# Moving the sums of a layer norm from VectorE to ScalarE in 36 of 64 gates

## The chip, the cores and the metric

The kernel runs on one core of a Trainium2 chip, in float32. A core has a matrix engine (TensorE, "PE" in the profile; its weight loads are shown apart as "PEld"), three engines for elementwise work (VectorE "DVE", ScalarE "ACT", GpSimd "POOL"), and SyncE ("SP"), which issues transfers. Each engine works through a queue of its own, in order; the engines wait for each other through semaphores. The metric is the device time of one execution in microseconds (us). The time before is 2115.55 us, the median of three runs (2112.75, 2115.55, 2115.77).

## The reference

64 graphs of 256 nodes with 256 features each go through two layers of a graph network, each closed by a layer norm over the features. Cut to what matters:

```python
def _layernorm(x, axis=-1, eps=1e-5):
    m = jnp.mean(x, axis=axis, keepdims=True)
    v = jnp.var(x, axis=axis, keepdims=True)
    return (x - m) / jnp.sqrt(v + eps)

# layer 0: normalized adjacency times x times W, residual, norm
x = _layernorm(x + L0(x, adj, W, b, alpha))

# layer 1: a convolution over the nodes, message passing, and a GRU cell, residual, norm
h = relu(bn1(conv1d(x, conv1_w)))                      # 1 tap
x_conv = relu(bn2(conv1d(h, conv2_w)) + x)             # 17 taps
A = exp(-dist(x @ w_se.T + b_se)) * adj
x_nmp = A @ relu(x @ w_msg.T + b_msg)
x_in = concatenate([x_conv, x_nmp])
gi = x_in @ w_ih.T + b_ih
gh = x @ w_hh.T + b_hh
r, z = sigmoid(gi_r + gh_r), sigmoid(gi_z + gh_z)
n = tanh(gi_n + r * gh_n)
x = _layernorm(x + (1 - z) * n + z * x)
```

The change concerns the last line alone: how the mean and the variance of each node's 256 features are formed.

## The kernel before

**Quarters.** The 64 graphs are worked on in four quarters of 16 (Q). The convolution of 17 taps is done in a frequency domain: each graph is cut into 8 tiles of 32 nodes and transformed by matmuls, and a quarter's 16 x 8 tiles fill 128 partitions. So each quarter goes through: `layer0` and `layer1` graph by graph (layer1 ends in the tile's transform and in `xn_d`, the message-passing result in DRAM); 12 frequency steps (matmuls L548, whose weights `u` are streamed from DRAM by SP; the results are taken out of PSUM by ScalarE, L590, and VectorE, L592 and L593); an inverse transform, which is VectorE's work alone (L598, L630, L735 and their like); and then the gates, one GRU cell per graph.

**The gate stage.** `gru(g)` (L858) works on one graph in four pieces, each ended by a `yield`, at which other work may be put between. Its matrix product is formed by seven products of three matmuls of 384 columns each (L874), after a scheme of Strassen's kind, so sums of the inputs are needed beside them; POOL makes these (`sums`, L845) for the next graph. VectorE adds the products into `G` (L891, L892, L901, L903, L941), ScalarE copies two of them (L885, L894) and takes the tanh (L916, L932), VectorE does the arithmetic of the gates (`finished`, L924 to L934). L934 leaves the value to be normed in the tile that the profile calls `x_g` (256 nodes as 128 partitions x 2 chunks x 256 features). The input of the next graph gets its two relu passes on ScalarE in piece 3 (`transposed`, L823 or L831).

**The norm.** `normed` (L849) calls `layernorm` (L319): per chunk VectorE's statistics (`bn_stats` L326) and their aggregate (`bn_aggr` L327), then for both chunks the variance plus eps (L328, VectorE), the power -1/2 (L329, POOL), minus mean times that (L332, VectorE), and on ScalarE the application (L334). L852 issues the store of the result on ScalarE's queue. It is a generator with a halt after L329: `finished` runs it up to there, `ended()` (L854) runs the rest, in piece 3 of the next graph's gate, ahead of that graph's own load of x1 (`load_x1`, L801, on SP's queue). The tile for x1, which becomes `x_g`, has two buffers.

**Where gates run.** `gates(q, part)` chains gates. The first four of each quarter (EARLY, L772) run beside the layers of the next quarter's graphs. Gates 4 to 15 of the first three quarters are put into the next quarter's work: up to two in the frequency steps (pieces of a gate between steps), then `paced` beside the inverse transform (for each marked instruction of the main stream so many pieces of the other one are put behind it; RATES, L1096), and what is left beside the layers of the quarter after. The last quarter's 16 gates run alone at the end. The gates that stand fully beside the last quarter's inverse transform are 37 to 44.

**What sets the order.** The order of the calls is a program order; a scheduler then orders each engine's queue by its own estimates, and only `tc.issue_after` fixes places. So the order in a queue may differ from that of the text.

Of the kernel before, what the change touches and what calls it, by code (L numbers as in the profile page):

```python
# [9 lines left out]
F32 = mybir.dt.float32  # L10
AF = mybir.ActivationFunctionType
ALU = mybir.AluOpType
AX = mybir.AxisListType

P = 128
LN_EPS = 1e-5
# [10 lines left out]
def kernel(  # L27
# [27 lines left out]
    nc = tc.nc  # L55
    B, N, D = x.shape
# [3 lines left out]
    NCH = N // P  # L60
# [7 lines left out]
    Q = P // GT  # L68
# [11 lines left out]
    small = ctx.enter_context(tc.tile_pool(name="small", bufs=4))  # L80
# [4 lines left out]
    def accbank(name):  # L85
        return psacc.tile([P, 512], F32, tag="acc", name=name)
# [4 lines left out]
    def mark(op, gates=0):  # L91
        marks.append((op.ins, gates))
# [27 lines left out]
    unused = const.tile([P, N], F32, name="unused")  # L120
    neg_half = const.tile([P, 4], F32)
# [197 lines left out]
    def layernorm(y, eps=LN_EPS):  # L319

        chunks = range(y.shape[1])
        st = small.tile([P, NCH, nc.vector.BN_STATS_DIM], F32, name="ln_st")
        mv = small.tile([P, NCH, nc.vector.BN_AGGR_DIM], F32, name="ln_mv")
        rs = small.tile([P, NCH], F32, name="ln_rs")
        for c in chunks:
            nc.vector.bn_stats(st[:, c, :], y[:, c, :])  # L326
            nc.vector.bn_aggr(mv[:, c, :], st[:, c, :])  # L327
        nc.vector.tensor_scalar(rs[:, : len(chunks)], mv[:, : len(chunks), 1], eps, None, op0=ALU.add)  # L328
        nc.gpsimd.tensor_tensor(rs[:, : len(chunks)], rs[:, : len(chunks)], neg_half[:, : len(chunks)], op=ALU.pow)  # L329
        yield  # L330
        mr = small.tile([P, NCH], F32, name="ln_mr")
        nc.vector.scalar_tensor_tensor(mr[:, : len(chunks)], mv[:, : len(chunks), 0], -1.0, rs[:, : len(chunks)], op0=ALU.mult, op1=ALU.mult)  # L332
        for c in chunks:
            nc.scalar.activation(  # L334
                y[:, c, :], y[:, c, :], AF.Identity, bias=mr[:, c : c + 1], scale=rs[:, c : c + 1]
            )
# [435 lines left out]
    EARLY = 4  # L772
# [19 lines left out]
    def load_gate(g):  # L792
        inputs = GATE[g] = gate.tile([P, 3 * DCH, N], F32, name="inputs")
        nc.sync.dma_start(inputs[:, : 2 * DCH], xn_d[g])
        if in_blocks(g):
            with nc.allow_non_contiguous_dma("one channel"):
                nc.sync.dma_start(inputs[0:1, 0], x1_d[g // Q][g % Q][:, 0:1].rearrange("n d -> d n"))

    def load_x1(g):
        OWN[g] = gate.tile([P, NCH, D], F32, name="x1_g")  # L800
        nc.sync.dma_start(OWN[g], x1_d[g // Q][g % Q].rearrange("(c p) d -> p c d", p=P))  # L801

    def sent(g):


        if not in_blocks(g):
            residual(g)
# [6 lines left out]
    def transposed(g):  # L814

        inputs = GATE[g]
        xcT = inputs[:, 2 * DCH :]
        if in_blocks(g):
            behind(nc.vector.transpose(xcT.rearrange("p k (s r) -> p k s r", r=RB), CONV.pop(g)))
            nc.gpsimd.tensor_tensor(xcT, xcT, inputs[:, 0 : 2 * DCH : 2 * DCH - 1], op=ALU.add)  # L820
            nc.gpsimd.memset(inputs[0:1, 0], 1.0)
            for k in range(DCH):
                nc.scalar.activation(xcT[:, k], xcT[:, k], AF.Relu, bias=bn2_bias[:, k : k + 1])  # L823
            return
        xc = CONV.pop(g)
        p = bank("p_xcT").rearrange("p (k n) -> p k n", k=DCH)
        for k in range(DCH):
            for c in range(NCH):
                nc.tensor.transpose(p[:, k, c * P : (c + 1) * P], xc[:, c, k * P : (k + 1) * P], ident)
        for k in range(DCH):  # L830
            nc.scalar.activation(xcT[:, k], p[:, k], AF.Relu, bias=bn2_bias[:, k : k + 1])  # L831

    def halves(inputs):

        return [inputs[:, i * HALF : (i + 1) * HALF, c * P : (c + 1) * P] for c in range(2) for i in range(2)]
# [10 lines left out]

    NORMS = []

    def normed(g, part, y):  # L849

        yield from layernorm(y, 4 * LN_EPS)
        nc.scalar.dma_start(out[g].rearrange("(c p) d -> p c d", p=P)[:, part], y)  # L852

    def ended():  # L854
        while NORMS:
            run(NORMS.pop(0))

    def gru(g):  # L858

        following = g % Q + 1 < Q
        inputs, S = GATE.pop(g), SUMS.pop(g)
        G = gate.tile([P, NCH, 2, 4, HD], F32, name="G", bufs=1)
        if following:
            load_gate(g + 1)
        A11, A12, A21, A22 = halves(inputs)

        def product(a, b, p=None):
            first = p is None  # L870
            if first:
                p = accbank("p_g")
            for k in range(HALF):
                nc.tensor.matmul(  # L874
                    p[:, : 3 * HD] if k == 0 else p[:, HD:], a[:, k], wall[:, b, k].rearrange("p t d -> p (t d)"),
                    start=first and k == 0, stop=True, skip_group_check=not first or k > 0,
                )
            return p

        def quarter(c, h):  # L880
            return G[:, c, h].rearrange("p t d -> p (t d)")

        p1 = product(A11, B11)
        first = gate.tile([P, 4 * HD], F32, name="first", bufs=1)
        nc.scalar.copy(first, p1)  # L885
        p7 = product(S[3], T3)
        yield
        if following:
            sent(g + 1)
        p6 = product(S[2], T2)  # L890
        mark(nc.vector.tensor_add(quarter(0, 1), first, p6), 1)  # L891
        nc.vector.tensor_add(quarter(1, 1), quarter(0, 1), p7)  # L892
        product(A12, B21, p1)
        nc.scalar.copy(quarter(0, 0), p1)  # L894
        yield
        if following:
            transposed(g + 1)
        ended()
        load_x1(g)
        p5 = product(S[1], T1)  # L900
        mark(nc.vector.tensor_add(quarter(1, 1), quarter(1, 1), p5), 1)  # L901
        product(A22, T4, p7)
        mark(nc.vector.tensor_add(quarter(1, 0), quarter(0, 1), p7), 1)  # L903
        if following:
            input_sums(g + 1, 3, 1, 2)
        yield
        product(S[4], B22, p5)
        if following:
            input_sums(g + 1, 4)
        if g % Q + 2 < Q:  # L910
            load_conv(g + 2)
        x1 = OWN.pop(g)

        def squashed(c):
            rz = G[:, c, :, GR : GZ + 1, :].rearrange("p h t d -> p h (t d)")
            nc.scalar.activation(rz, rz, AF.Tanh, scale=0.5)  # L916

        squashed(1)

        def finished(part):  # L920
            both = G[:, part].rearrange("p c h t d -> p (c h) t d")
            chunks = both.shape[1] // 2
            r, z, n, i = (both[:, :, j, :] for j in (GR, GZ, GN, GI))
            nc.vector.scalar_tensor_tensor(n, r, 1.0, n, op0=ALU.add, op1=ALU.mult)  # L924
            i4 = i.rearrange("p (c h) d -> p c h d", h=2)
            bias = bn_t.rearrange("p (h d) -> p h d", h=2).unsqueeze(1).to_broadcast([P, chunks, 2, HD])
            nc.vector.tensor_tensor(i4, i4, bias, op=ALU.add)
            nc.vector.scalar_tensor_tensor(i, n, 0.5, i, op0=ALU.mult, op1=ALU.add)  # L928
            y = x1[:, part]
            yq = y.rearrange("p c (h d) -> p (c h) d", h=2)  # L930
            mark(nc.vector.scalar_tensor_tensor(yq, z, 3.0, yq, op0=ALU.add, op1=ALU.mult), 1)  # L931
            nc.scalar.activation(i, i, AF.Tanh)  # L932
            nc.vector.scalar_tensor_tensor(i, z, 1.0, i, op0=ALU.subtract, op1=ALU.mult)  # L933
            nc.vector.tensor_sub(yq, yq, i)  # L934
            NORMS.append(normed(g, part, y))
            next(NORMS[-1])

        if g == B - 1:
            finished(slice(1, 2))
            ended()  # L940
        mark(nc.vector.tensor_add(quarter(0, 1), quarter(0, 1), p5), 1)  # L941
        squashed(0)
        finished(slice(0, 1 if g == B - 1 else NCH))
        yield
# [26 lines left out]
    def run(stage):  # L971
        for _ in stage:
            pass
# [137 lines left out]
    for q in range(NQ):  # L1111
# [46 lines left out]
        else:  # L1158
            run(gates(q, range(Q)))
    ended()  # L1160
    order.close()

# [52 lines left out]
```

## Time and profile before

| | |
|---|---|
| median of three runs | 2115.55 us |
| the profiled execution, its own time | 2121.38 us |
| its span, first to last instruction | 2119.6 us |
| granted clock of TensorE, mean | 0.986 |
| PE busy | 2012.2 us (95%) |
| VectorE busy | 1463.9 us (69%) |
| ScalarE busy | 906.1 us (43%) |
| POOL busy | 671.3 us (32%) |

The profiled execution took 5.8 us longer than the median. Busy times are sums over instructions of one engine; an engine's instructions can overlap a little at their ends, so that the distance from one start to the next can be shorter than a duration. From the rows of the frequency products and of the gate products in the trace: the frequency steps of the four quarters run at about 299 to 400, 632 to 741, 1140 to 1254 and 1645 to 1725 us, the first gates start near 530 us, the last quarter's own gates run from about 1895 us to the end. The stages of a gate can be told by the lines: L874 for the products, L845 for the sums, L934 for the finished `x_g`, L326 to L334 for its norm.

In rows of the timeline the columns are: start (us), duration (us), engine, line, operation, output<-inputs with their shapes; in brackets the idle time of the engine before it and what it waited for. In rows of the waits: engine, the tile waited on, the line, what released it, and then the idle time in us, how many waits, and the longest.

### The profile page before, as it was taken

What the parts mean: (1) busy time and instruction counts of PE and PEld (TensorE: products, weight loads), DVE (VectorE), ACT (ScalarE), POOL (GpSimd) and SP (SyncE); (2) the same over time, 40 slices, a digit from 0 to 9 for tenths busy, and PEclk for the clock granted to TensorE, in tenths of its full rate; (3) what the DMA queues carried; (4) which work ended last, traced back from release to release, by engine and by line L of the source; (5) the groups of instructions that cost most, each with busy time, mean ns of one, the idle gap of its engine ahead of it and who ended that gap; (6) DMA issues with size and microseconds to landing.
All of it is one profiled execution on the core that took longest, in us unless ns stands there. A gap on an engine that the chain in (4) does not pass through costs nothing. (4 is left out here: it accounts for less than half of the span.)

```text
span 2119.6 us, 26193 instructions
## 1 busy us (share of the span) xinstructions
PE 2012.2 (95%) x8157; PEld 1448.3 (68%) x8157; DVE 1463.9 (69%) x3333; ACT 906.1 (43%) x2128; POOL 671.3 (32%) x672
## 2 busy tenths in 40 slices
PE   6999899999999999999999999999999999999997
PEld 5888678877667756767667765667767765555554
DVE  5555368676468788873546888885444889976776
ACT  4666543477431233555453123455444123333333
POOL 3445310121431243323221233332322124334453
PEclk9999899999999999999999999999999999999999
DMA  4765556545437644344325654434332855443331
GB/s 122 221 221 186 156 164 224 173 135 157 129 106 220 200 128 119 124 121 119 95 90 157 202 173 125 134 108 126 100 90 80 250 152 149 115 116 94 95 95 55
DMA packets 305289, 298.05 MB, mean 141 GB/s; under 512 B 84192, under 2 KB 283956, under 8 KB 305150
## 3 DMA queue, kind: packets, MB, share of 16 engines
q1 hardware_dynamic: 245198, 200.37, 32.3%
q10 hardware_dynamic: 44480, 67.39, 8.9%
q0 software_dynamic: 15472, 28.61, 6.1%
q8 instruction: 66, 1.08, 0.2%
q14 instruction: 73, 0.60, 0.1%
HBM read 193.19 MB, written 103.06 MB: 140 GB/s over the span
## 5 line engine op out<-in xcount | busy, mean ns | idle before, releaser
L874 PE MATMUL p_g<-wall,sums 128*128 128x384 f32 x1536 | 538.8, 491 | 7.2 <-DVE G L901 7.2
L874 PE MATMUL p_g<-wall,inputs 128*128 128x384 f32 x1152 | 407.4, 490 | 14.3 <-DVE G L892 14.3
L874 PEld LDWEIGHTS p_g<-wall,sums 128*128 128x128 f32 x1536 | 285.2, 191 | 197.5 <-issue 16.7
L874 PEld LDWEIGHTS p_g<-wall,inputs 128*128 128x128 f32 x1152 | 217.2, 191 | 166.8 <-DVE G L892 23.8
L845 POOL TENSOR_TENSOR sums<-inputs 128x384 f32<-128x384 f32 x128 | 139.5, 1090 | 342.4 <-PE p_g L874 314.0
L329 POOL TENSOR_TENSOR ln_rs<-ln_rs,neg_half 128x2 f32<-128x2 f32 x129 | 95.0, 737 | 391.4 <-DVE ln_rs L328 303.5
L916 ACT ACTIVATE G<-G 128x512 f32<-128x512 f32 x128 | 80.9, 632 | 263.1 <-DVE G L903 144.1
L548 PE MATMUL p_k<-u,VM 128*128 128x256 f32 x736 | 175.8, 381 | 2.4 <-DMA u<-ud 2.4
L548 PEld LDWEIGHTS p_k<-u,VM 128*128 128x128 f32 x736 | 139.4, 191 | 29.4 <-issue 2.7
L400 PE MATMUL p_hT<-adjT,x 128*128 128x256 f32 x512 | 129.9, 397 | 11.1 <-ACT msg L474 6.2
L370 POOL TENSOR_TENSOR dis<-deg,neg_half 128x2 f32<-128x2 f32 x64 | 47.3, 738 | 290.4 <-DVE deg L368 290.0
L450 PE MATMUL p_conv<-wc,xn 128*128 128x259 f32 x512 | 128.2, 391 | 11.5 <-DVE xn L434 10.6
L393 POOL TENSOR_TENSOR x_t<-x_t,b_t 128x512 f32<-128x512 f32 x64 | 94.4, 1476 | 135.8 <-issue 111.4
L410 PE MATMUL p_out<-w,hT 128*128 128x256 f32 x512 | 126.3, 390 | 1.8 <-ACT hT L405 1.3
L486 PE MATMUL p_dft<-fwd,h 128*128 128x240 f32 x512 | 117.0, 372 | 11.2 <-ACT scols L454 11.2
L522 PE MATMUL p_nmp<-aT,msg 128*128 128x256 f32 x512 | 122.6, 382 | 0.5 <-DVE aT L515 0.5
L450 PEld LDWEIGHTS p_conv<-wc,xn 128*128 128x128 f32 x512 | 96.3, 192 | 38.2 <-DVE xn L434 15.5
L471 PE MATMUL p_msg<-wmsg,xn 128*128 128x256 f32 x512 | 121.6, 380 | 0.0
L334 ACT ACTIVATE x_g<-x_g,ln_mr,ln_rs 128x256 f32<-128x256 f32 x128 | 71.0, 597 | 112.0 <-DVE ln_mr L332 110.2
L410 PEld LDWEIGHTS p_out<-w,hT 128*128 128x128 f32 x512 | 97.8, 194 | 29.4 <-ACT hT L405 9.5
L845 POOL TENSOR_TENSOR sums<-inputs,sums 128x384 f32<-128x384 f32 x64 | 69.1, 1079 | 146.6 <-PE p_g L874 146.3
L400 PEld LDWEIGHTS p_hT<-adjT,x 128*128 128x128 f32 x512 | 96.0, 198 | 27.9 <-ACT msg L474 10.9
(163 smaller groups left out, 3545.5 us busy)
## 6 DMA issues: line engine op xcount, KB each, us to landing
u<-ud SPq DMA_DIRECT2D x284, 256.0 KB
xn_d<-xn ACTq DMA_DIRECT2D x64, 512.0 KB
inputs<-xn_d SPq DMA_DIRECT2D x64, 512.0 KB
ud<-u_set POOLq DMA_DIRECT2D x39, 480.0 KB, 6.7
adj_t<-in_adj_dram SPq DMA_DIRECT2D x64, 256.0 KB
x_t<-in_x_dram SPq DMA_DIRECT2D x64, 256.0 KB
x_d<-x ACTq DMA_DIRECT2D x64, 256.0 KB
xc_d<-VM SPq DMA_DIRECT2D x64, 256.0 KB
```

The lines of the kernel that those rows point to most:

```text
L329: nc.gpsimd.tensor_tensor(rs[:, : len(chunks)], rs[:, : len(chunks)], neg_half[:, : len(chunks)], op=ALU.pow)
L393: nc.gpsimd.tensor_tensor(x_t, x_t, b0_t.unsqueeze(1).to_broadcast([P, NCH, D]), op=ALU.add)
L400: nc.tensor.matmul(p[:, k, :], x1[:, mc, k * P : (k + 1) * P], adjT[:, mc, 1 - mc : 3 - mc, :].rearrange("p n q -> p (n q)"), start=mc == ...
L410: nc.tensor.matmul(p[:, c, :], hT[:, k, c * P : (c + 1) * P], w0[:, k, :], start=k == 0, stop=k == DCH - 1)
L450: nc.tensor.matmul(p, x1T[:, k, c * P : (c + 1) * P], wc1[:, k, :], start=k == 0, stop=k == DCH - 1)
L471: nc.tensor.matmul(p[:, c, :], x1T[:, k, c * P : (c + 1) * P], wmsg[:, k, :], start=k == 0, stop=k == DCH - 1)
L486: nc.tensor.matmul(p[:, t0 * FL : t1 * FL], h[:, c, k * P : (k + 1) * P], fwd[:, first : first + t1 - t0, :].rearrange("p t f -> p (t f)") ...
L522: nc.tensor.matmul(p[:, k, :], msg[:, mc, k * P : (k + 1) * P], aT[:, mc].rearrange("p n q -> p (n q)"), start=mc == 0, stop=mc == NCH - 1,)
L548: nc.tensor.matmul(p[:, j * D : (j + 1) * D], v[:, k, :], u[:, k, :], start=k == 0, stop=k == DCH - 1)
L845: nc.gpsimd.tensor_tensor(S[i], x, y, op=op)
L874: nc.tensor.matmul(p[:, : 3 * HD] if k == 0 else p[:, HD:], a[:, k], wall[:, b, k].rearrange("p t d -> p (t d)"), start=first and k == 0, ...
L916: nc.scalar.activation(rz, rz, AF.Tanh, scale=0.5)
```

## The change

In gates 4 to 15 of the first three quarters (36 of 64) the statistics are formed by ScalarE: a Copy with scale -1/256 whose accumulator gives minus the mean, and a Square with that as its bias whose accumulator gives the sum of squared deviations, both per chunk, so four passes over 128x256 elements. VectorE then makes the variance plus eps from the sums (one instruction for both chunks, as before), POOL takes the power, VectorE multiplies minus mean by it, and ScalarE applies both. The passes' full results go to a tile `unused`, the same that the sums of degrees in `layer0` write. The norms of the other 28 gates are formed as before.

The places in the program order change too. For the 36 gates `finished` no longer runs any part of the norm; `measured()`, which stands where `ended()` stood in piece 3 of the next graph's gate, runs the statistics up to the power; `ended()` now stands in piece 4, behind the last product, and runs the rest. For the other 28 gates `measured()` runs the rest of `layernorm` at the old place, and only the store of the result moves to the new place of `ended()`.

```diff
--- before.py
+++ after.py
@@ -846,14 +846,43 @@
 
     NORMS = []
 
+    def scalar_statistics(y, eps):
+
+        sums = small.tile([P, 2, NCH], F32, name="ln_sums")
+        rs = small.tile([P, NCH], F32, name="ln_rs")
+        mr = small.tile([P, NCH], F32, name="ln_mr")
+        for c in range(NCH):
+            nc.scalar.activation(unused, y[:, c, :], AF.Copy, scale=-1.0 / D, accum_out=sums[:, 0, c : c + 1])
+        for c in range(NCH):
+            nc.scalar.activation(
+                unused, y[:, c, :], AF.Square, bias=sums[:, 0, c : c + 1], accum_out=sums[:, 1, c : c + 1]
+            )
+        nc.vector.tensor_scalar(rs, sums[:, 1], 1.0 / D, eps, op0=ALU.mult, op1=ALU.add)
+        nc.gpsimd.tensor_tensor(rs, rs, neg_half[:, :NCH], op=ALU.pow)
+        yield
+        nc.vector.tensor_mul(mr, sums[:, 0], rs)
+        for c in range(NCH):
+            nc.scalar.activation(
+                y[:, c, :], y[:, c, :], AF.Identity, bias=mr[:, c : c + 1], scale=rs[:, c : c + 1]
+            )
+
     def normed(g, part, y):
 
-        yield from layernorm(y, 4 * LN_EPS)
+        if EARLY <= g % Q and g < B - Q:
+            yield
+            yield from scalar_statistics(y, 4 * LN_EPS)
+        else:
+            yield from layernorm(y, 4 * LN_EPS)
+            yield
         nc.scalar.dma_start(out[g].rearrange("(c p) d -> p c d", p=P)[:, part], y)
 
     def ended():
         while NORMS:
             run(NORMS.pop(0))
+
+    def measured():
+        for norm in NORMS:
+            next(norm, None)
 
     def gru(g):
 
@@ -895,7 +924,7 @@
         yield
         if following:
             transposed(g + 1)
-        ended()
+        measured()
         load_x1(g)
         p5 = product(S[1], T1)
         mark(nc.vector.tensor_add(quarter(1, 1), quarter(1, 1), p5), 1)
@@ -905,6 +934,7 @@
             input_sums(g + 1, 3, 1, 2)
         yield
         product(S[4], B22, p5)
+        ended()
         if following:
             input_sums(g + 1, 4)
         if g % Q + 2 < Q:
```

In the changed file the new instructions have these lines: L855 (Copy), L857 (Square), L860 (variance), L861 (power), L863 (product), L865 (application); L877 issues the store. The other lines of a gate move down by about 30 (L874 becomes L903, L892 becomes L921, L934 becomes L964).

## The prediction

> **What bounds the kernel now.** I read the page first, then a table of stages, then the timeline of one gate, then the waits of TensorE (PE).
>
> The page's first two parts: busy time of each engine, and VectorE (DVE) in 40 slices of 53 us.
>
> ```profile
> PE 2012.2 (95%) x8157; PEld 1448.3 (68%) x8157; DVE 1463.9 (69%) x3333; ACT 906.1 (43%) x2128; POOL 671.3 (32%) x672
> ...
> DVE  5555368676468788873546888885444889976776
> ```
>
> PE is the bound over the whole, at 95%. ScalarE (ACT) looks free at 43%. But DVE has two slices at 9: the mean of 69% hides a stretch where it is full. The stage table shows which:
>
> ```profile
> core 0: us, PE busy (x) PEld busy (x) DVE busy (x) ACT busy (x) POOL busy (x), PEclk, DMA share, GB/s
> ...
> 742.00:848.00 106.00, 103.84 (x370) 65.07 (x369) 91.79 (x187) 39.84 (x85) 41.99 (x40) 1.00 0.44 123
> ...
> 1725.00:1857.00 132.00, 121.98 (x395) 70.32 (x393) 131.52 (x257) 40.13 (x75) 56.02 (x50) 1.00 0.46 118
> 1943.00:2106.00 163.00, 162.60 (x504) 95.87 (x505) 115.06 (x216) 60.62 (x108) 74.53 (x80) 1.00 0.35 90
> ```
>
> Three stretches with gates in them. From 742 to 848 changed gates run beside transform pieces and a few layers: PE 104 of 106. From 1725 to 1857 eight changed gates (37 to 44) run beside the last transform: DVE 131.5 of 132, PE 122. From 1943 to 2106 run twelve of the last 16 gates, which keep VectorE's statistics: PE 162.6 of 163. So only the 132 us in the middle are DVE's; a gate takes 15.6 us there (x_g finished at 1742.34 and, seven gates on, at 1851.22) against 163/12 = 13.6 us where PE sets the pace.
>
> One gate of that stretch (38), from its finished x_g to the next gate's third sum; the ends overlap, so I go by starts:
>
> ```profile
> 1757.86 0.68 DVE L934 TENSOR_TENSOR x_g<-x_g,G 128x512 f32<-128x512 f32 x1
> ...
> 1758.65 0.59 ACT L894 COPY G<-p_g 128x512 f32<-128x512 f32 x1 [1.99 <-DVE x_g L934]
> 1758.80 0.74 DVE L326 BATCH_NORM_STATS2 ln_st<-x_g 128x6 f32<-128x256 f32 x2
> ...
> 1759.46 0.16 DVE L327 BATCH_NORM_AGGREGATE ln_mv<-ln_st 128x2 f32<-128x6 f32 x1
> ...
> 1760.11 0.17 DVE L327 BATCH_NORM_AGGREGATE ln_mv<-ln_st 128x2 f32<-128x6 f32 x1
> ...
> 1760.78 0.16 DVE L328 TENSOR_SCALAR ln_rs<-ln_mv 128x2 f32<-128x2 f32 x1
> ...
> 1761.02 0.72 POOL L329 TENSOR_TENSOR ln_rs<-ln_rs,neg_half 128x2 f32<-128x2 f32 x1 [5.57 <-DVE ln_rs L328]
> ...
> 1761.58 2.20 PE L874 MATMUL p_g<-wall,inputs 128*128 128x384 f32 x6 [1.20 <-DVE G L892]
> 1761.72 1.29 POOL L845 TENSOR_TENSOR sums<-inputs 128x384 f32<-128x384 f32 x1
> 1762.05 0.97 DVE L332 SCALAR_TENSOR_TENSOR ln_mr<-ln_mv,ln_rs 128x2 f32<-128x2 f32 x1
> 1762.94 0.68 DVE L901 TENSOR_TENSOR G<-G,p_g 128x512 f32<-128x512 f32 x1
> ```
>
> Three things are to be seen. DVE never idles: while POOL takes the power (L329, 0.72), DVE does other work. L332, two elements wide, takes 0.97 us and ends with POOL's sum (1761.72 + 1.29 = 1763.01): it stood behind it. And PE waited 1.20 us for L892. In this stretch PE's waits are
>
> ```profile
> PE p_g L874 <- DVE G L892: 7.0, 6, 1.6
> PE p_g L874 <- DVE G L901: 2.9, 2, 1.7
> ```
>
> **What goes.** 36 gates (4 to 15 of the first three quarters) lose two L326 and two L327. From start to start that is 0.66 + 0.08 + 0.09 = 0.83 us of DVE per gate (busy 1.16, but overlapped). Over the eight gates of the full stretch: 8 x 0.83 = 6.6 us, the prize. L328 and L332 have successors (L860, L863) and stay.
>
> **What comes.** Four ACT passes over 128x256 per gate, each with an accumulator read. The nearest rows are the degree sums, back to back, and a pass with a bias column:
>
> ```profile
> 983.92 0.42 ACT L357 ACTIVATE unused<-adj_t 128x256 f32<-128x256 f32 x1
> 984.24 0.19 ACT L357 ACTIVATION_READ_ACCUMULATOR unused<-adj_t 128x1 f32 x1
> 984.47 0.42 ACT L357 ACTIVATE unused<-adj_t 128x256 f32<-128x256 f32 x1
> 984.79 0.19 ACT L357 ACTIVATION_READ_ACCUMULATOR unused<-adj_t 128x1 f32 x1
> ```
>
> ```profile
> L823 ACT ACTIVATE inputs<-inputs,bn_bias 128x256 f32<-128x256 f32 x56 | 26.1, 504 | 52.4 <-POOL inputs L820 52.4
> ```
>
> A Copy with its read takes 0.55 from start to start; a Square with a bias 0.50 + 0.19 less 0.06 of overlap, 0.63. Per gate 2 x 0.55 + 2 x 0.63 = 2.36 us, 85 us in all, on an engine 30% busy in the full stretch (40.13 of 132).
>
> On the text of the program this is "a graph later". In the queues as built it is not: the four passes stand directly behind the tanh of the same gate, and wait only for its x_g. So I write s for the start of the op that finishes x_g. ACT starts at s + 0.79 (1757.86 to 1758.65 above), ends at s + 3.15. VectorE's L860 can start at s + 3.20; POOL's power follows 0.24 later (1760.78 to 1761.02), lasts 0.72; L863 starts at s + 4.2. DVE's own queue between x_g and L860 holds 2.2 to 3.1 us of work after s + 0.60. So:
>
> - Before L860, DVE idles about 0.35 us in gates 39, 42 and 44 and 0.1 in 43: 1.15. In gates 37 and 41 one copy and two relu passes (0.49 + 0.76 = 1.25, by starts) stand between the last two Squares; L860 is late there by 1.3 and 0.7: 2.0.
> - Between L860 and L863, before, two to four ops covered the power. Now none in gates 38, 40, 41 and 42 (0.93 idle each, 3.7), one in 43 and two in 39 and 44 (0.3 each, 0.9), three in 37.
> - L860 and L863 themselves: 0.17 x 8 = 1.4.
> - The wait behind POOL's sum. Bounds: nothing (L332 took 0.16 at its median) to the whole sum, 1.0 per gate. The sum now also waits for the two relu passes, which end at about s + 5.0, when L863 may be through; but then the transform piece behind L930 meets it instead. I take 0.5 per gate, 4.0, and 0.4 more in gate 41.
>
> Sum 13.6. The same items before: 0.83 + 0.07 (L328) + 0.68 (L332, mean 0.76 less overlap) = 1.58, times 8 is 12.6. **The full stretch: +1.0 us**; the 6.6 us are paid back as waits. With no idle it would be 13.6 - 7.75 = 5.85, so -6.8; with 0.35 of idle before L860, 0.93 before L863, a whole sum of 1.0 and L860 and L863 at 0.17 together in every gate, 8 x 2.45 = 19.6, so +7.0.
>
> **The other places.** Gate 6 (and 22) stands in the frequency steps; its L860 and L863 follow x_g directly, and behind them L592, which empties PSUM. From s = 737.44: passes to 741.1 (one copy of 0.5 between), L860 at 741.15, L863 at 742.15, L592 at 742.3 instead of 741.47. PE waits for L901 soon after (0.38 us), so it passes on: 2 x 0.85 = **+1.7** (bounds 0 and 2 x 1.9).
>
> Gate 47, before the last quarter: PE waited 0.34 for L901 behind an L332 of 0.95. The new chain ends at about the same time or 1 us later: **+0.5**.
>
> Relief: elsewhere in the first two gate stretches PE waits for L892 three times each, 2.5 and 3.8 us; L892 now comes 0.83 earlier, at most 6 x 0.83 = 5.0. I take **-2.0**, since half of these waits are under 0.83.
>
> Gates beside layers (some 7): 0.83 less DVE, 2.36 more ACT between copies that layers wait for. Bounds -0.83 and +1.25 each; I take 0, as both engines idle there.
>
> The stores of all gates are issued after the product S4, behind no new DMA; x_g has two buffers, and on SP's queue its next load stands most of a graph later. POOL's power moves at most a few tenths against its sums, which PE needs 5 us later (sum done 1764.1, used after 1768). Both at nothing; the cover is that slack.
>
> Sum: 1.0 + 1.7 + 0.5 - 2.0 = **+1.2 us**. The profiled execution took 2121.38 us (span 2119.6), 5.8 above the median of 2115.55; I add the sum to the median: **2117**.
>
> A page weighed: "ScalarE: Activation LUTs", in its rules for kernel authors, tells one to give adds and multiplies to VectorE, not ScalarE, which speaks against the change. The same page's section on the table load puts a pass at 186 ns + 0.833 N, and 93 ns for a bias column: 399 and 492 ns for N = 256, an estimate that the rows (417, 504) bear out, but it has no accumulator read. By the page four passes would take 1.8 us, the 1.15 us of idle before L860 would be gone, and the sum near 0.
>
> **Rivals.** *Faster: DVE's relief is kept.* For: DVE is full and PE has 10 us of slack there. Price: -6.8, and a third of the 19 us that PE waits for DVE in 636 to 954 and 1113 to 1431 (9.4 and 9.9): -13, 2102.5 at best, some -8 typically. Against: four gates have nothing between L860 and L863. It decides if ACT's chain is under 2.2 us.
>
> *Slower: ScalarE's chain is what VectorE waits for.* One mechanism: L860 and L863 head DVE's queue while ACT, then POOL, work. Price: +7.0 in the full stretch, 2 x 1.9 in the steps, +0.5: +11.3, 2127. It decides once idle and lock pass 1.6 us per gate.
>
> *SP.* The store of x_g comes up to 1.5 us later (gate 6), its buffer's next load holds SP, and the u loads behind it are late. The chain has such DMA waits of 5.5 and 3.7 us. Six places by 1.5: +9, 2124.5. Against: the next x_g load comes over 5 us later.
>
> *The change is not what it says.* As told, "a graph later" is gone in the queues; this is in the sum. Square could have needed another table; the program as built has one table load, as before.
>
> **Numbers.** No net change (within 0.2%, 4.2 us, about what a measurement can tell): 0.38; faster 0.26; ScalarE's chain 0.30; SP 0.06. So slower 0.36. For 8 in 10 the range reaches to -9.5 and +11.5: 2106 to 2127; the likeliest case alone is 2111 to 2120.
>
> **What would show it.** After: DVE idle put down to L863 waiting for POOL, 0.9 in about half of the gates, and to L860 waiting for ACT; DVE's busy time 42 us lower (36 x 1.16) and 1725 to 1857 as long as before; ACT near 1000. Wrong if that stretch shrinks by 5 us or more (lock or ACT cheaper than taken), or if PE gets new waits for ACT copies beside layers.

## The result and the profile after

The changed kernel takes 2122.45 us (median, 2118.91 to 2131.01) where the kernel before takes 2115.83 us (2110.29 to 2123.07) on the same chip: a ratio of 1.0036 with a 95% interval of 1.002 to 1.0051, some 7.6 us slower. On a second chip it was 1.0036 again (1.0019 to 1.0052; 2119.14 against 2110.49 us). The prediction had 2117 us and a range of 2106 to 2127; its likeliest case, no change within 0.2%, did not come true.

The page of the changed kernel, engines and VectorE in 40 slices:

```profile
PE 2008.4 (95%) x8157; PEld 1445.3 (68%) x8157; DVE 1447.2 (68%) x3189; ACT 979.6 (46%) x2416; POOL 677.5 (32%) x672
...
DVE  5555368776468788863546978875444889977776
```

VectorE has 144 instructions fewer, but its busy time fell by 16.7 us, not by the 42 that 36 gates at 1.16 make: so its other instructions became longer. The stages, with the columns of before (length, busy time and count per engine, clock, DMA share, GB/s):

```profile
742.00:848.00 106.00, 102.68 (x372) 65.78 (x371) 91.02 (x169) 56.20 (x149) 43.87 (x42) 1.00 0.47 127
...
1725.00:1857.00 132.00, 120.54 (x389) 69.00 (x388) 125.43 (x217) 52.34 (x129) 50.64 (x47) 1.00 0.45 116
```

In the full stretch VectorE is no longer busy without a break (125.43 of 132). What it waits for there (waits of VectorE, 1726 to 1858 us: waiter, tile, line, releaser; us in all, times, longest):

```profile
DVE VM L592 <- PE p_k L548: 4.8, 1, 4.8
DVE ln_mr L863 <- POOL ln_rs L861: 4.2, 6, 0.8
DVE ln_rs L860 <- ACT unused L857: 1.5, 4, 0.9
```

The first is the end of the frequency steps; the kernel before waits there too (3.1 us). The other two are new: 5.7 us. One gate of the stretch (40) in the timeline:

```profile
1790.28 0.68 DVE L964 TENSOR_TENSOR x_g<-x_g,G 128x512 f32<-128x512 f32 x1
...
1790.99 0.42 ACT L855 ACTIVATE unused<-x_g 128x256 f32<-128x256 f32 x1 [1.92 <-DVE x_g L964]
...
1793.12 0.19 ACT L857 ACTIVATION_READ_ACCUMULATOR unused<-x_g,ln_sums 128x1 f32 x1
...
1793.76 0.15 DVE L860 TENSOR_SCALAR ln_rs<-ln_sums 128x2 f32<-128x2 f32 x1
...
1793.99 0.72 POOL L861 TENSOR_TENSOR ln_rs<-ln_rs,neg_half 128x2 f32<-128x2 f32 x1 [6.73 <-DVE ln_rs L860]
1794.69 0.98 POOL L845 TENSOR_TENSOR sums<-inputs 128x384 f32<-128x384 f32 x1
1794.74 0.95 DVE L863 TENSOR_TENSOR ln_mr<-ln_sums,ln_rs 128x2 f32<-128x2 f32 x1 [0.83 <-POOL ln_rs L861]
...
1795.62 0.68 DVE L930 TENSOR_TENSOR G<-G,p_g 128x512 f32<-128x512 f32 x1
...
1796.44 2.17 PE L903 MATMUL p_g<-wall,sums 128*128 128x384 f32 x6 [1.35 <-DVE G L930]
```

Here L860 and L863 stand next to each other in VectorE's queue; so they do in gates 38, 40, 41 and 42 of the eight from 37 to 44, where in the kernel before two to four other instructions stood between L328 and L332. So VectorE stands still while POOL takes the power (0.83 us), then L863, two elements wide, starts just after a sum of POOL and is held until that ends (0.95), and TensorE waits 1.35 us for the L930 behind both.

Where the time went, by stage. The lengths run from the finished `x_g` of one gate to that of another, or to the adjacency product L515 of a graph; a quarter's frequency steps begin and end at L593, VectorE's last work on a step (the first of the three begins at x_g of gate 3), and gates 7 to 15 and 23 to 31 are counted from there. What TensorE's clock lost in them (the sum over windows of 1 us of one minus the granted clock) is taken off, except between gates 37 and 44, where VectorE sets the time.

| us | before | changed | changed, second trace |
|---|---|---|---|
| frequency steps of the last three quarters | 289.9 | 291.3 | 289.5 |
| gates 7 to 15 and 23 to 31 | 407.1 | 409.0 | 409.0 |
| handovers: gate 15 to graph 42, gate 31 to graph 57 | 142.1 | 149.5 | 147.1 |
| layers from there to the next steps | 238.4 | 236.4 | 235.5 |
| gates 37 to 44 | 108.9 | 112.6 | 112.6 |
| gates 44 to 51 | 99.3 | 97.2 | 98.3 |

Two rows carry the loss: the full stretch, +3.7, and the handovers, where the last late gate of a quarter meets the first early gates of the next, +5.0 to +7.4. The layers' row runs over work that the change leaves alone; it shows how far two executions differ. Each column is one execution: at the handovers, a kernel of the experiments below that leaves them as they were measured 143.7 us, 1.6 above the kernel before.

The full stretch can be summed from start to start on VectorE (time from each instruction's start to the next one's, less idle), for the seven gates from x_g of 37 to x_g of 44: statistics L326 and L327 gone, -5.84 us (0.83 per gate); L860 and L863 against L328 and L332, 4.28 against 5.92, -1.64; idle +5.78; and +5.37 on all other instructions, which are the same. The sum is the +3.67 measured.

### The profile page after: what moved, and what is told of

The parts are those of the page before. It is cut to its first block, busy times and chain, and to the rows that moved or that the text cites. A ratio compares the mean times of both kernels' runs of the same rounds, so it can differ in the third digit from the quotient of the medians.

```text
span 2122.0 us, 26356 instructions
## 1 busy us (share of the span) xinstructions
PE 2008.4 (95%) x8157; PEld 1445.3 (68%) x8157; DVE 1447.2 (68%) x3189; ACT 979.6 (46%) x2416; POOL 677.5 (32%) x672
## 5 line engine op out<-in xcount | busy, mean ns | idle before, releaser
L903 PE MATMUL p_g<-wall,sums 128*128 128x384 f32 x1536 | 537.3, 490 | 13.9 <-DVE G L930 13.9
L903 PEld LDWEIGHTS p_g<-wall,sums 128*128 128x128 f32 x1536 | 284.4, 190 | 204.6 <-POOL sums L845 15.8
L903 PE MATMUL p_g<-wall,inputs 128*128 128x384 f32 x1152 | 405.1, 487 | 7.8 <-DVE G L921 7.8
L903 PEld LDWEIGHTS p_g<-wall,inputs 128*128 128x128 f32 x1152 | 216.7, 190 | 157.7 <-DVE G L921 15.1
L845 POOL TENSOR_TENSOR sums<-inputs 128x384 f32<-128x384 f32 x128 | 146.5, 1145 | 340.4 <-PE p_g L903 319.9
L329 POOL TENSOR_TENSOR ln_rs<-ln_rs,neg_half 128x2 f32<-128x2 f32 (+1 forms) x93 | 67.7, 728 | 292.9 <-DVE ln_rs L328 179.0
L845 POOL TENSOR_TENSOR sums<-inputs,sums 128x384 f32<-128x384 f32 x64 | 71.5, 1118 | 129.3 <-PE p_g L903 127.8
L486 PEld LDWEIGHTS p_dft<-fwd,h 128*128 128x128 f32 x512 | 96.2, 191 | 24.2 <-ACT scols L454 15.8
```

Source lines behind the costliest of these rows:

```text
L486: nc.tensor.matmul(p[:, t0 * FL : t1 * FL], h[:, c, k * P : (k + 1) * P], fwd[:, first : first + t1 - t0, :].rearrange("p t f -> p (t f)") ...
L845: nc.gpsimd.tensor_tensor(S[i], x, y, op=op)
L903: nc.tensor.matmul(p[:, : 3 * HD] if k == 0 else p[:, HD:], a[:, k], wall[:, b, k].rearrange("p t d -> p (t d)"), start=first and k == 0, ...
```

## The experiments

Theory A after the result: the loss is made of VectorE's stalls in the full stretch, and of another order of the queues at the handovers. Rival B: it is the new places in the program, whatever engine forms the sums. Rival C: it is ScalarE's passes, which get in the way of other ScalarE work. The first expectations give the handovers per place, up to graphs 38 and 54; the results give both together, up to graphs 42 and 57 as in the table.

**The places without ScalarE.** VectorE's statistics in all gates, at the changed kernel's places:

```diff
         if EARLY <= g % Q and g < B - Q:
             yield
-            yield from scalar_statistics(y, 4 * LN_EPS)
+            yield from layernorm(y, 4 * LN_EPS)
```

> All 64 gates keep VectorE's statistics; the 36 gates only take them, and apply them, at the changed kernel's places in the program. Theory A (stalls in the full stretch, and a changed order of ScalarE's queue where the last late gate of a quarter meets the first early one): from the finished x_g of gate 37 to that of gate 44 it takes 108.9 us as in the kernel before (112.6 in the changed one), but the two handovers (finished x_g of gate 15 to the adjacency product of graph 38, gate 31 to graph 54) take 14.8 us as in the changed kernel, not 13.0: in all +3.6 us, ratio 1.0017. Rival B (the places alone cost the time, not the engine): as slow as the changed kernel, 1.0036. Rival C (only ScalarE's passes cost): 1.000, handovers 13.0.

Measured: 2129.76 against 2111.05 us, 1.0079 (1.0049 to 1.0109): by the medians slower than the changed kernel itself. Gates 37 to 44 take 115.0 us, gates 7 to 15 and 23 to 31 414.4, the handovers 146.6. Theory A missed here and rival C fell. VectorE's waits between those gates:

```profile
DVE ln_mr L332 <- POOL ln_rs L329: 3.3, 4, 0.8
```

There was no such wait in this stretch before. With the two halves called in pieces 3 and 4 the scheduler put L328 and L332 side by side in five of the eight gates. So the place is what costs; ScalarE's sums at the same places gave part of it back by the medians, 1.0079 to 1.0036.

**The full stretch alone.** `if 37 <= g <= 44:` in place of the condition.

> ScalarE's sums in gates 37 to 44 alone, the stretch where VectorE is full. Theory A: 112.6 us between x_g of gates 37 and 44, with 5 to 6 us of VectorE's idle put down to L863 and L860; handovers 13.0; +3.7 us, ratio 1.0017. Rival (this stretch gives its loss back in the gates behind it): 1.000 although the stretch is 112.6.

Measured: 2111.06 against 2111.05 us, 1.0006 (0.9985 to 1.0027). The stretch took 112.3 us with the same two waits (4.2 and 1.5 us), but gates 44 to 51 98.1 instead of 99.3. The stretch's loss is as expected. In the whole it is under what the runs can tell: the interval holds 1.0017 as well as the rival's 1.000, and 1.2 of the 3.4 us came back in the gates behind.

**The handovers.** The last gate of a quarter (15, 31, 47) as in the kernel before, the other 33 as changed, and the reverse: only those three take VectorE's statistics at the changed places.

```diff
-        if EARLY <= g % Q and g < B - Q:
+        if EARLY <= g % Q < Q - 1 and g < B - Q:
```

> As the changed kernel, but the last gate of each quarter (15, 31, 47) keeps VectorE's statistics at the old place. Theory A: both handovers 13.0 us again, gates 37 to 44 still 112.6: +4 us, ratio 1.0019. Rival (the handovers are no cause but a place where lost time shows): 1.0036.

```diff
-        if EARLY <= g % Q and g < B - Q:
+        if g % Q == Q - 1 and g < B - Q:
             yield
-            yield from scalar_statistics(y, 4 * LN_EPS)
+            yield from layernorm(y, 4 * LN_EPS)
```

> VectorE's statistics in all gates; only the last gate of the first three quarters (15, 31, 47) takes them late, at the changed kernel's places. If the order of the queues at the handovers costs by itself, whatever engine forms the sums: from the finished x_g of gate 31 to the adjacency product of graph 57 65 us at full clock instead of 60.9, from gate 15 to graph 42 83 instead of 81, gates 46 to 48 1 us longer, in all 5 to 8 us, ratio 1.0025 to 1.004. Rival (it takes ScalarE's passes there, or the queues make up for it): 1.000, 60.9 and 81.

Measured: without the three gates 2109.38 against 2111.05 us, 0.9986 (0.9966 to 1.0007), handovers 143.7 us together, gates 37 to 44 112.5; with these three alone 2110.84 against 2110.49, 1.0016 (0.9998 to 1.0034), handovers 147.5 (gate 15 to graph 42 83.8, gate 31 to graph 57 63.8), gates 44 to 51 95.6. The handovers went as theory A has it; both totals are under what was expected, 1.0019 and 1.0025. In both kernels gates 44 to 51 are shorter than before, by 4.4 us (94.9) and 3.7 us, which I had not expected. Taking these three gates out moves the ratio from 1.0036 to 0.9986, by more than the whole loss, and alone they come to 1.0016; so they are a large part of the loss, but how large the runs do not settle.

What happens there is seen behind gate 15. The changed kernel's timeline:

```profile
944.79 3.22 PE L450 MATMUL p_conv<-wc,xn 128*128 128x259 f32 x8 [3.11 <-DVE xn L434]
...
952.50 1.27 POOL L820 TENSOR_TENSOR inputs<-inputs 128x512 f32<-128x512 f32 x1
...
953.80 0.51 ACT L823 ACTIVATE inputs<-inputs,bn_bias 128x256 f32<-128x256 f32 x1 [1.82 <-POOL inputs L820]
954.21 0.46 ACT L491 COPY VM<-p_dft 128x384 f32<-128x384 f32 x1
954.57 0.36 ACT L501 COPY dist_l<-p_rows 64x256 f32<-64x256 f32 x1
...
954.97 0.43 DVE L506 COPY dist_r<-p_rows 64x256 f32<-64x256 f32 x1 [4.00 <-ACT dist_l L501]
...
955.45 0.70 PE L513 MATMUL p_dist<-dist_r,dist_l 32*128 32x256 f32 x4 [1.23 <-DVE dist_r L506]
```

and the kernel before, the same instructions:

```profile
947.07 3.68 PE L450 MATMUL p_conv<-wc,xn 128*128 128x259 f32 x8 [2.40 <-DVE xn L434]
...
954.59 0.48 ACT L491 COPY VM<-p_dft 128x384 f32<-128x384 f32 x1 [0.33 <-PE p_dft L486]
...
954.97 0.37 ACT L501 COPY dist_l<-p_rows 64x256 f32<-64x256 f32 x1
955.23 0.51 ACT L823 ACTIVATE inputs<-inputs,bn_bias 128x256 f32<-128x256 f32 x1
955.37 0.43 DVE L506 COPY dist_r<-p_rows 64x256 f32<-64x256 f32 x1 [2.27 <-ACT dist_l L501]
...
956.43 0.70 PE L513 MATMUL p_dist<-dist_r,dist_l 32*128 32x256 f32 x4
```

A relu pass of the next early gate (L823) now stands in ScalarE's queue ahead of the copies L491 and L501 that the layer needs. It waits 1.82 us for POOL's L820, which stands behind three sums; VectorE waits 4.00 us for L501, and TensorE 1.23 us for VectorE. Before, L823 came behind both copies. L434, the input of TensorE's next product, is also later (3.11 against 2.40 us of waiting), behind the layer's own statistics. Behind gate 31 it is the same (3.09 against 2.40, and 1.29 for L506 against none). The queues of the kernel with only these three gates moved have the new order too, those of the kernel without them the old one.

These two waits come to 3.9 us at both places together, of the +5.0 to +7.4; what the rest is, no run shows. And the place of L823 is only a part: in the kernel below in which only the product is moved, L491 and L501 stand ahead of that L823 again and TensorE has no wait for L506, but it still waits 3.1 us for L434, and the handovers take 146.2 us.

**The passes left out.** L855 and L857 go; L860 and L863 read two elements of `x_g`, so the norm of these gates is without meaning.

```diff
-        for c in range(NCH):
-            nc.scalar.activation(unused, y[:, c, :], AF.Copy, scale=-1.0 / D, accum_out=sums[:, 0, c : c + 1])
...
-        nc.vector.tensor_scalar(rs, sums[:, 1], 1.0 / D, eps, op0=ALU.mult, op1=ALU.add)
+        nc.vector.tensor_scalar(rs, y[:, 0, :NCH], 0.0, eps, op0=ALU.mult, op1=ALU.add)
...
-        nc.vector.tensor_mul(mr, sums[:, 0], rs)
+        nc.vector.tensor_mul(mr, y[:, 0, :NCH], rs)
```

> As the changed kernel without ScalarE's four passes: variance and mean are taken from two elements of x_g, so the norm of the 36 gates is without meaning; all other instructions stay, the wait for the power too. Theory A: only the idle before L860 goes (1.5 us in gates 37 to 44: 111), the idle before L863 stays or grows: ratio 1.000 to 1.002. Rival C (the passes delay ScalarE's copies for the layers and the gates): 0.997 or less, and the handover of gate 31 at 13.0.

Measured: 2113.85 against 2110.61 us, 1.0014 (0.9999 to 1.0029), gates 37 to 44 109.9 with 4.8 us of idle before L863, the handovers 147.1, as long as with the passes: rival C falls there too. In the stretch the passes account for 2.7 us (112.6 to 109.9). But even with no statistics at all, neither on VectorE nor on ScalarE, the changed places are no gain: what the statistics cost VectorE before (5.84 us in the stretch) is eaten by the wait for the power and by POOL's sums.

**The two halves apart.** First only the product with the mean (L863) and the application moved, behind the next graph's last sum; then also the variance and the power (L860, L861), behind its third sum; then the same places for the product with VectorE's statistics, taken directly behind `x_g` as in the kernel before. In all three the application on ScalarE and the store move along with the product; they were not moved apart from it.

```diff
         product(S[4], B22, p5)
-        ended()
...
-        mark(nc.vector.tensor_add(quarter(0, 1), quarter(0, 1), p5), 1)
+        added = nc.vector.tensor_add(quarter(0, 1), quarter(0, 1), p5)
+        mark(added, 1)
+        with tc.issue_after(added.ins):
+            ended()
```

> As the changed kernel, only the product with the mean and the application behind the next graph's last sum; variance and power stay directly behind ScalarE's sums. Theory A: of VectorE's idle in gates 37 to 44 the part before L863 (4.2 us) goes and that before L860 (1.5) stays: 109 us instead of 112.6; ratio 0.997 to 1.000. Rival (the wait for ScalarE's sums counts as much elsewhere, 14.6 us in 18 places): 1.002 or more.

```diff
+        yield
         nc.vector.tensor_scalar(rs, sums[:, 1], 1.0 / D, eps, op0=ALU.mult, op1=ALU.add)
...
-        mark(nc.vector.tensor_add(quarter(1, 1), quarter(1, 1), p5), 1)
+        added = nc.vector.tensor_add(quarter(1, 1), quarter(1, 1), p5)
+        mark(added, 1)
+        with tc.issue_after(added.ins):
+            measured()
```

> As the changed kernel, but the variance and the power are put behind the next graph's third sum in VectorE's queue, and the product with the mean and the application behind that graph's last sum, so that the sums are really used a graph later. Theory A: VectorE's idle in gates 37 to 44 falls from 5.8 to under 1 us, the stretch from 112.6 to 107 (105 if POOL's sums hold up VectorE no longer than before); handovers still 14.8; ratio 1.0036 less 5.5 us: 1.0010. Rival (VectorE's other work is held up by POOL's sums for as long as it idled): stretch 110 or more, ratio 1.002 or more.

```diff
         if EARLY <= g % Q and g < B - Q:
-            yield
-            yield from scalar_statistics(y, 4 * LN_EPS)
+            norm = layernorm(y, 4 * LN_EPS)
+            next(norm)
+            yield
+            yield
+            yield
+            run(norm)
```

> VectorE's statistics stay in all gates, taken and raised to the power directly behind x_g as in the kernel before; only the product with the mean and the application are put a graph later, behind the next graph's last sum. Theory A (the gain of the covered kernel is that VectorE no longer stands behind POOL's power; the engine of the sums is of no matter): 17.5 us of such waits in 24 places go, gates 37 to 44 108.9, ratio 0.993 to 0.995. Rival D (it is VectorE's relief, 0.83 us in 36 gates, once nothing takes it back): 0.998 or more, gates 37 to 44 108.9 or more.

| | time, before beside it (us) | ratio (95%) | gates 37 to 44 | steps | gates 7 to 15, 23 to 31 |
|---|---|---|---|---|---|
| product moved | 2094.63, 2110.61 | 0.9925 (0.9902 to 0.9947) | 109.3 | 284.0 | 403.2 |
| product, variance and power moved | 2094.30, 2111.05 | 0.9916 (0.9886 to 0.9947) | 107.7 | 283.8 | 404.5 |
| VectorE's statistics, product moved | 2096.24, 2110.61 | 0.9934 (0.9909 to 0.996) | 105.9 | 287.5 | 403.2 |

All three are faster than the kernel before, with ScalarE or without it. The stretch went as expected in the first two (109, 107) and 3.0 us better in the third (108.9 expected); the whole gained more than expected in the first two (0.997 to 1.000 and 1.0010 expected), with 3 to 6 us each in stages where TensorE was thought to be the bound: steps 289.9 to 284, gates 7 to 15 and 23 to 31 407 to 404, gates 44 to 51 99.3 to 93.4. Over the whole changed kernel VectorE waits 19.3 us for the power before L863 and 18.2 us for ScalarE's sums before L860. With the product alone moved the first are gone and 15.4 us of the second stay, and the kernel is as fast as with both covered: it is the wait for the power that counts. The waits of VectorE between gates 37 and 44 with all of it moved:

```profile
DVE ln_mr L864 <- POOL ln_rs L862: 0.7, 1, 0.7
DVE G L937 <- PE p_g L905: 0.6, 1, 0.6
DVE ln_rs L861 <- ACT unused L857: 0.3, 1, 0.3
```

So rival B holds, in this form: outside the handovers the cost is the place of the product behind the power. That ScalarE forms the sums is worth 3.7 us in the frequency steps and costs 1.8 and 1.3 us in the other two columns; the ratios of the last two kernels cannot be told apart.

**POOL's sums left out.** To see what the +5.37 us on VectorE's other instructions are, the changed kernel without L845; the products read a part of the weights instead.

```diff
-            S[i] = gate.tile([P, HALF, P], F32, name=f"sums{i}", bufs=1)
+            S[i] = wall[:, i, :, 0, :]
...
-            nc.gpsimd.tensor_tensor(S[i], x, y, op=op)
```

> As the changed kernel without POOL's sums of the gates (the products take a part of the weights in their place, so the gates' results are without meaning; matmuls and all else stay). If VectorE is held up by these sums: of its 20 us of excess between gates 37 and 44 under 3 stay, and the 112.6 us shrink to what PE sets, 95 to 98; ratio 0.985 to 0.992. If the excess comes from elsewhere (the DMA that POOL issues, PSUM): it stays at 15 us or more and the stretch over 108.

Measured: 2069.16 against 2110.49 us, 0.9806 (0.9781 to 0.9831), more than expected; gates 37 to 44 97.0 us with TensorE busy throughout (window over that stretch):

```profile
1701.00:1798.00 97.00, 97.00 (x321) 58.10 (x320) 87.22 (x187) 48.79 (x119) 13.91 (x14) 1.00 0.55 147
```

Taking as excess what an instruction takes beyond the lower quartile of its operation and shape in the whole kernel, where that is over 0.05 us, VectorE has 17.6 us of it between gates 37 and 44 before, 20.1 in the changed kernel, and 0.0 here. On instructions other than the two small ones of the norm it is 12.8 before and 17.3 after: 4.5 of the +5.37 us. The first lines below are the changed kernel's groups of VectorE, 1743 to 1856 us, the second the same instructions without POOL's sums (lines one lower):

```profile
L958 DVE SCALAR_TENSOR_TENSOR G<-G 128x512 f32<-128x512 f32 x7 | 8.0, 1136 | 0.0
...
L638 DVE SCALAR_TENSOR_TENSOR turn<-VM 128x256 f32<-128x256 f32 x4 | 2.5, 614 | 0.0
```

```profile
L957 DVE SCALAR_TENSOR_TENSOR G<-G 128x512 f32<-128x512 f32 x7 | 4.8, 683 | 0.0
...
L638 DVE SCALAR_TENSOR_TENSOR turn<-VM 128x256 f32<-128x256 f32 x4 | 1.7, 417 | 0.0
```

**Combinations.** The product, variance and power moved, and gates 15, 31 and 47 as in the kernel before (on top of the edits of the kernel with all three moved):

```diff
-        if EARLY <= g % Q and g < B - Q:
+        if EARLY <= g % Q < Q - 1 and g < B - Q:
```

> The kernel with the sums really used a graph later, and the last gate of each quarter (15, 31, 47) with VectorE's statistics at the old place. If the order at the handovers costs by itself, the two gains add: handover of gate 31 (to the adjacency product of graph 57) 61.6 us instead of 63.3 at full clock, gates 37 to 44 still 107.7, ratio 0.990 against 0.9916 without this edit. Rival (with the product covered the handover costs nothing): 0.9916 again.

Measured: 2089.66 against 2110.61 us, 0.9902 (0.9877 to 0.9928); handovers 141.3 us together, gates 37 to 44 107.8. It is the fastest median of the kernels that form POOL's sums, though its interval meets that of 0.9916. Then ScalarE's sums only in gates 4 to 6, 20 to 22, 36, 45 and 46, VectorE's statistics in the other 24, the product moved in all 33:

```diff
-        if EARLY <= g % Q and g < B - Q:
+        if g in ON_SCALAR:
             yield
             yield from scalar_statistics(y, 4 * LN_EPS)
+        elif EARLY <= g % Q < Q - 1 and g < B - Q:
+            norm = layernorm(y, 4 * LN_EPS)
+            next(norm)
...
```

> Product with the mean and application a graph later everywhere (gates 15, 31 and 47 as in the kernel before); ScalarE forms the sums only in the gates in the frequency steps and in 45 and 46 (4 to 6, 20 to 22, 36, 45, 46), VectorE in the others. By the stages of the two covered kernels: the frequency steps as with ScalarE (103.4 and 104.1 us against 105.1 and 105.9), gates 7 to 12 and 23 to 28 as with VectorE (127.5 and 95.6 against 128.6 and 96.9), gates 37 to 44 106: some 4 us under the better of the two, ratio 0.988. If the stages only trade with one another: 0.990 or more.

Measured: 2092.45 against 2110.49 us, 0.9924 (0.99 to 0.9947). Gates 37 to 44 took 105.3 us as expected, but gates 7 to 12 128.5 and 23 to 28 96.5, as with ScalarE: the stages trade with one another, and choosing by stage gained nothing that can be measured.

**The changed kernel again**, on another chip:

> The changed kernel once more, beside the three others and the kernel before on one chip. Ratio 1.0036 as in the first comparison (interval 1.002 to 1.005); gates 37 to 44 112.6 us again. If the loss were of that first chip or of its clock, 1.000.

Measured: 1.0036 (1.0019 to 1.0052), gates 37 to 44 112.6 us, idle 5.7 us. The loss is not of one chip.

## Why the prediction was right and wrong

The prediction had 2117 us, +1.2 of sum, and called no change the likeliest; measured was +0.36% (0.2 to 0.51), some 7.6 us. The range held because its rivals had made it 21 us wide. The sum did not see the loss: it has nothing for the handovers, and it comes near zero in part by terms that did not come.

Right was where VectorE is the bound, and that "the 6.6 us are paid back as waits": 0.83 us per gate went (5.84 for seven), and idle of 5.78 came, against 6.8 for seven gates in the prediction (7.75 for eight). The split was off: before L860 1.5 us instead of 2.8, before L863 4.2 instead of 4.0. Which gates have none, one, two and three instructions between L860 and L863 was right in all eight. That the kernel does not do "a graph later" in its queues was right, and is what decides.

Wrong was, first, "the wait behind POOL's sum", taken at 0.5 per gate after and 0.68 before, as if it belonged to the two-element instruction. It belongs to the sum. In the full stretch 27 VectorE instructions were held by 0.2 us or more in the kernel before, six of them L332; in the changed one 28, three of them L863 and one L860. When the small instruction is not in the way, the next one is. (The two small instructions took 0.85 us per gate before, from start to start in these seven gates, where the sum has 0.75.) For seven gates, the two small instructions and this wait together were forecast at -0.2 us; with all that the wait reaches they came to 5.37 - 1.64 = +3.7. That is 3.9 more than forecast; added to the forecast for seven gates, +0.9, and less the 1.0 by which the idle was taken too high, it gives 3.8, the +3.7 of the stretch.

Second, "gates beside layers ... I take 0, as both engines idle there". The step counted the passes and not the order: gate 15's and gate 31's norm moved other instructions in three queues, and the handovers cost 5.0 to 7.4 us. The move of `ended()` and of the stores, costed "at nothing" with the slack of the transfers as cover, is part of this step: the cover named was for transfers, and what was late was a ScalarE copy behind a relu pass. What the step lacked is the order in which the queues were built. It is also what the prediction named as a sign of being wrong: TensorE has new waits for ScalarE's copies beside layers, 1.23 us behind gate 15 and 1.29 us behind gate 31, both by way of L506.

Third, the relief of -2.0 us for TensorE's waits in the first two gate stretches did not come; gates 7 to 15 and 23 to 31 took 1.9 us more. The +1.7 for the frequency steps, worked out for gates 6 and 22, has +1.4 and -0.4 in the two traces; the steps hold gates 4 to 6 and 20 to 22, not "up to two" gates as the section on the kernel before has it. Gate 47's +0.5 was of the right sign up to gate 48 (+0.9 and +2.3 in the two traces), but the gates behind it took 3 us less, so that 44 to 51 is 1.0 to 2.1 us shorter.

Of the rivals, the slower one named the right places (L860 and L863 at the head of VectorE's queue) and a price for the stretch of +7.0, of which 3.7 came; the handovers, the other part of the loss, it did not have. "Faster" was said to be decided by ScalarE's chain being under 2.2 us. The runs show something else decides: with the passes as they are, and variance, power and product put later, the kernel is 0.84% faster than before. The rival on SP's queue had 9 us; TensorE's waits for `u` in the last quarter's steps were 3.4 us against 1.7, and the three quarters' steps took +1.4 and -0.4.

## What to carry to other kernels

When work is moved from a full engine, look at what the rest of its chain does in that engine's queue: two small dependent instructions with another engine's step between them cost the full engine that step, unless independent work stands between them; placing the second one behind work that is due anyway was worth more here (0.7% without moving the sums, 0.8% with it) than moving the sums. Where one engine holds another, as POOL's sums held VectorE here, the stall is a price of the holding instruction and does not go away with the instruction that shows it: 17.6 us of it before, 20.1 after. And before a moved call is costed at nothing, read the queues as built where two streams meet, each queue for itself.

## What the runs showed of the hardware

**VectorE held by POOL.** Each of the 27 held instructions before, and of the 28 after, overlaps a sum L845, and ends a fixed time after the sum ends: 0.02 us for two elements, 0.28 for 256, 0.55 for 512. In the changed kernel:

```profile
1798.77 1.04 POOL L845 TENSOR_TENSOR sums<-inputs,sums 128x384 f32<-128x384 f32 x1 [0.29 <-PE p_g L903]
1798.87 1.22 DVE L638 SCALAR_TENSOR_TENSOR turn<-VM 128x256 f32<-128x256 f32 x1
```

L638 takes 0.41 us alone; started in a sum that ends at 1799.81, it ends at 1800.09, 0.28 us after it. Additions that read one of their operands from PSUM were not held (L941 in the kernel before, three times inside a sum: 0.67 to 0.68 us). The Trainium skill, "SBUF — State Buffer", section "SBUF: two separate sides", says that VectorE and GpSimd share a pair of ports as an exclusive lock for the whole instruction, which VectorE needs for two SBUF inputs or a two-port mode. The trace agrees, and gives the price: 0.6 to 0.7 us per sum in a stretch where VectorE is full (17.6 and 20.1 us in 28 sums). L860, with one input from SBUF, was held once too (0.58 us against 0.15); whether it runs in a two-port mode no run here shows.

**TensorE's clock falls behind a gap.** The changed kernel behind gate 15, windows of 1 us:

```profile
942.00:943.00 1.00, 0.00 (x0) 0.00 (x0) 1.00 (x3) 0.99 (x3) 0.00 (x0) 1.00 0.00 0
943.00:944.00 1.00, 0.00 (x0) 0.00 (x0) 1.00 (x3) 0.17 (x1) 0.70 (x1) 1.00 0.92 356
...
946.00:947.00 1.00, 1.00 (x4) 0.73 (x3) 0.79 (x1) 0.65 (x3) 1.00 (x2) 0.50 0.55 90
947.00:948.00 1.00, 1.00 (x4) 0.70 (x3) 0.16 (x1) 0.64 (x2) 1.00 (x2) 0.50 0.35 52
```

TensorE stands still from 941.7 to 944.8 us, and then runs at half clock from 945.4 to 948.9. Such a fall loses 1.7 us of clock, or twice that (8 of 63). In all fourteen traces, from 290 to 2090 us, 18 of 20 gaps of 2.9 us and more between matmuls were followed by one, 30 of 55 of 2.2 to 2.9, and 11 of 85 of 1.5 to 2.2; four falls came with no gap of 1.5 us just ahead of them. So the gap of 2.4 us behind gate 15 costs 1.7 us in the kernel before and nothing in four of the experiments' kernels that have it too, which is why a stage can differ that much between two traces, and a stall of 3 us costs nearly 5. The Trainium skill, "TensorE: Matmul & The Clock Gate", Part 1, tells of a free-running activity window of about 3.4 us and a clock of one half behind an idle one; 1.7 us lost is half of such a window, and a share that rises with the gap's length fits a window that is not tied to the gap. But the page asks for an idle window, and gaps of 1.6 to 2.4 us were enough here at times; by the traces TensorE need not be idle for the whole of it. That the window is what decides is argued, not shown.
